# Keys of the last context made between the first scores of an attention, its values four units earlier, and one set of value copies moved to ScalarE

## The chip, the cores and the metric

The kernel runs on one core of a Trainium2 chip. The metric is device time in microseconds; before the change it is 987.43 us, the median of 3 runs (987.35 to 987.92). Engines are named as in the profile: PE (TensorE, matmul), PEld (its weight loads), DVE (VectorE), ACT (ScalarE), POOL (GpSimd), SP (the queue that issues most DMAs).

## The reference

Two layers over x of 4 batches x 512 tokens x 256 features. Each layer is an attention over a context of 1024 rows per batch and then a feed-forward with experts. The change touches the attention of the second layer and the keys and values that are made for it:

```python
# layer 1, attention (x is layer-normed first, the result is added to x)
q = (x @ Wq).reshape(B, N, H, D).transpose(0, 2, 1, 3)        # 4 heads of 64
kv = (context @ Wkv).reshape(B, M, 2, H, D).transpose(2, 0, 3, 1, 4)
k, v = (kv[0], kv[1])
attn = jnp.einsum('bhnd,bhmd->bhnm', q, k) * SCALE
attn = jnp.where(mask[:, None, :, :], attn, -jnp.inf)
attn = jax.nn.softmax(attn, axis=-1)
out = jnp.einsum('bhnm,bhmd->bhnd', attn, v)
out = out.transpose(0, 2, 1, 3).reshape(B, N, C) @ Wo
```

The feed-forward of layer 0 picks the best 2 of 12 experts for each token (8 with weights, 4 that pass the token through), that of layer 1 the best 2 of 8. All is float32.

## The kernel before

The kernel is one program in five stages: the attention of layer 0 with the routing of its tokens, the experts of layer 0, the attention of layer 1 with the routing of its tokens, four expert tiles of layer 1 ahead of time, and the experts of layer 1.

**Order of the work.** PE runs in the order in which the program is written (`manual_schedule` for PE); in the expert stages SP does too. On DVE, ACT and POOL a scheduler sets the order when the program is built, and each of these engines then runs its instructions strictly in that order. Buffers come from pools that take a tile whose last reader is done: two PSUM buffers for ordinary matmul results (`mm_ps`), two for transposes (`tr_ps`), two of two banks for scores (`score_ps`), and six of about 8 KB a partition in SBUF (`t8`) for keys, values, mask biases, row buffers and expert weights.

**Keys and values.** `mha_kv` (lines 464 to 499) is a generator that makes one batch's keys in four pieces and its values in four more. A key piece is two matmuls of 128x128 by 128x512 (L475), each in two passes, into one `mm_ps` buffer; it is copied to SBUF by ACT (L480) for the first half of the context and by DVE (L482) for the second. A value piece is four matmuls of 128x128 by 128x256 (L489); its copy goes to DVE (L495) for even pieces and to ACT (L497) for odd ones, except for batch 2, where ACT does all. `mha_kvs` chains batches. Batches 0 and 1 are made in `layer0_experts`, between the last routing steps and the first expert tile, batch 2 after the experts. Batch 3 is made inside the second attention.

**The experts of layer 0.** `moe` runs over tiles of 128 rows. For a tile `i`, `turn` forms the rows' destinations `to` on DVE (L1051, needs the rows' DMA) and transposes the rows on PE (`ht`, L1060); `up` is the first matrix (`hp`, L1085), `down` the second (`y`, L1110). Three ring slots hold expert weights; SP reloads a slot when PE has left it.

**The second attention.** `layer1_attention` (L653) goes over 32 units of (batch, 128 tokens, pair of heads), eight to a batch. Unit `i` issues: its scores (`s`, L587), whose softmax is one reduction on DVE and one exponential on ACT for each of the two heads (L596, L600); the transposes of the first head of unit `i - 2` (`a2t`, L610, copied out by DVE L613 and ACT L615); for units 11 to 18 a piece of batch 3's keys or values; the output projection (`wo`, L650) of unit `i - 4`, when it is the second pair; the values product (`o`, L635) of unit `i - 3`; a step of routing and a piece of the next batch's queries, where one is due; and last the transposes of the second head of unit `i - 2`. The scores of a unit need the score buffers of the unit before, which DVE's reduction frees. Batch 3's keys are first read in unit 24. The routing of a finished batch starts at units 11, 19 and 27 and after the last, the next batch's queries at units 0, 8 and 16, so that units eight apart lie at the same place in both.

Of the kernel before, what the change touches and what calls it, by code (L numbers as in the profile page):

```python
# [60 lines left out]
def two_layers(ctx: ExitStack, tc: tile.TileContext, io, out):  # L61
# [14 lines left out]
    def t8(shape, name, dt=F32):  # L76
        return k8.tile(shape, dt, tag="k8", name=name)
# [16 lines left out]
    def mm_ps(name):  # L94
        return ps_m.tile([P, 512], F32, tag="m", name=name)
# [41 lines left out]
    def after(a, b, why):  # L137
        info = mybir.DependencyInfo(mybir.DependencyClass.Sync, mybir.DependencyReason.DATA)
        tc.add_manual_dep(a.ins, b.ins.name, info, reason=why)
# [53 lines left out]
    for e in range(EX):  # L193
        i = nc.gpsimd.dma_start(
            out=rows[e * REGION : (e + 1) * REGION, :].rearrange("(p k) r -> p k r", p=P),
            in_=zeros.unsqueeze(1).to_broadcast([P, REGION // P, ROW]),
        )
# [264 lines left out]
    def ctx_room(k, shape, name):  # L462
        return res.tile(shape, F32, tag=f"ctxT{k}", name=name)

    def mha_kv(b, st):


        kT = ctx_room(0, [P, NC, M], "kT_2") if b == 2 else t8([P, NC, M], f"kT_{b}")
        for n in range(NC):
            for h in range(2):  # L470
                if n + h > 0:
                    yield
                op = mm_ps(f"k_{b}_{n}_{h}")
                for c in range(NC):
                    nc.tensor.matmul(  # L475
                        op, wkv[:, c, bass.ts(n, P)], ctxT[b][:, c, bass.ts(h, 512)],
                        start=(c == 0), stop=(c == NC - 1),
                    )
                if h == 0:
                    nc.scalar.copy(kT[:, n, bass.ts(h, 512)], op)  # L480
                else:
                    copied = nc.vector.tensor_copy(kT[:, n, bass.ts(h, 512)], op)  # L482
        v = ctx_room(1, [P, NJ, D], "v_2") if b == 2 else t8([P, NJ, D], f"v_{b}")
        for g in range(NJ // 2):
            yield
            op = mm_ps(f"v_{b}_{g}")
            for k in range(2):
                for c in range(NC):
                    nc.tensor.matmul(  # L489
                        op[:, bass.ts(k, D)], ctxT[b][:, c, bass.ts(2 * g + k, P)], wkv[:, c, D : 2 * D],  # L490
                        start=(c == 0), stop=(c == NC - 1),
                    )
            d = v[:, 2 * g : 2 * g + 2, :].rearrange("p j n -> p (j n)")
            if g % 2 == 0 and b != 2:
                nc.vector.tensor_copy(d, op)  # L495
            else:
                nc.scalar.copy(d, op)  # L497
        st.update(b=b, kT=kT, v=v, copied=copied)
        yield

    def mha_kvs(sts, bs):
        for b in bs:
            sts[b] = {}
            yield from mha_kv(b, sts[b])
# [6 lines left out]
    def mha_bias(st, t):  # L511

        if t == 0:
            st["mbias"] = t8([P, NT, M], f"mbias_{st['b']}", BF16)
        return nc.vector.tensor_scalar(
            st["mbias"][:, t, :], st["mask"][:, t, :], 1.0, MASKED, ALU.subtract, ALU.mult
        )
# [62 lines left out]
    def mha_scores(st, n, t):  # L580

        b = st["b"]
        sps = [score_ps(f"s2_{b}_{n}_{t}_{r}") for r in range(2)]
        for k in range(2):
            for r in range(2):
                at = slice(r * HD, r * HD + HD)
                nc.tensor.matmul(  # L587
                    sps[r][:, k, :], st["qT"][at, n, bass.ts(t, P)], st["kT"][at, n, bass.ts(k, 512)],
                    start=True, stop=True,
                )  # L590
        ps = []
        tot = sm.tile([P, 2], F32, tag="s2_tot", name=f"s2_tot_{b}_{n}_{t}", bufs=6)
        for r in range(2):
            p = t4([P, M], f"p2_{b}_{n}_{t}_{r}")
            nm = tsmall([P, 1], "s2_nm")
            nc.vector.tensor_tensor_reduce(  # L596
                p, sps[r].rearrange("p h n -> p (h n)"), st["mbias"][:, t, :],
                -ATT_SCALE, -ATT_SCALE * LEAST, ALU.add, ALU.min, nm,
            )
            nc.scalar.activation(p, p, AF.Exp, bias=nm, scale=-1.0, accum_out=tot[:, r : r + 1])  # L600
            ps.append(p)
        st["unit"] = nc.vector.reciprocal(tot, tot)
        return ps, tot
# [13 lines left out]
    def mha_turns(st, n, t, ps):  # L617
        b = st["b"]
        aT = tbig(f"a2T_{b}_{n}_{t}").rearrange("p (r k) s -> p r (k s)", r=2)
        for r, p in enumerate(ps):  # L620
            yield aT
            mha_turn(aT[:, r, :], p, f"a2t_{b}_{n}_{t}_{r}", r)
        yield
# [22 lines left out]
    def mha_out(st, t):  # L646
        b = st["b"]
        op = mm_ps(f"wo_{b}_{t}")[:, 0:D]
        for c in range(NC):
            nc.tensor.matmul(op, st["oT"][:, c, :], wo[:, c, :], start=(c == 0), stop=(c == NC - 1))  # L650
        nc.vector.tensor_tensor(x[b][:, t, :], op, x[b][:, t, :], ALU.add)

    def layer1_attention(sts):  # L653

        units = []
        for b in range(NB):
            units += [(b, t, n) for t in range(NT) for n in range(NC)]
        ps, aTs = {}, {}  # L660
        route, queries = None, None
        kvs = mha_kvs(sts, (NB - 1,))
        done = None
        for i in range(len(units) + 4):
            if i < len(units):
                b, t, n = units[i]
                ps[i] = mha_scores(sts[b], n, t)
                unit = sts[b]
                if i + 1 < len(units) and units[i + 1][0] > 0 and units[i + 1][2] == 0:
                    bias = mha_bias(sts[units[i + 1][0]], units[i + 1][1])  # L670
                    after(bias, done, "a piece to a unit")
                done = sts[b]["unit"]
            if 0 <= i - 2 < len(units):
                b, t, n = units[i - 2]
                turns = mha_turns(sts[b], n, t, ps[i - 2][0])
                aTs[i - 2] = next(turns)
                next(turns)
            if 11 <= i < 19:
                next(kvs)
            if 0 <= i - 4 < len(units):  # L680
                b, t, n = units[i - 4]
                if n == NC - 1:
                    mha_out(sts[b], t)
            if 0 <= i - 3 < len(units):
                b, t, n = units[i - 3]
                mha_values(sts[b], n, t, aTs.pop(i - 3), ps.pop(i - 3)[1])
            if route:
                next(route, None)
            if pending:
                scatter_pending(2, unit["unit"] if i < len(units) else None)  # L690
            if queries:
                next(queries, None)
            if 0 <= i - 2 < len(units):
                next(turns)
            b = i // (2 * NT) + 1
            if b < NB and i % (2 * NT) == QUERIES:
                queries = mha_q_pieces(b, sts)
            if i == len(units) - 5:
                slots = slots_ahead()
            if i == len(units) - 3:  # L700
                tiles = tiles_ahead(slots, *load_ahead(), sts[NB - 1]["unit"])
            if i == len(units) + 2:
                next(tiles)
            b, k = divmod(i - 11, 2 * NT)
            if k == 0 and 0 <= b < NB:
                route = route_steps(L1, b)
                next(route)
        for n in PIECES:
            for _ in range(n):
                next(tiles, None)  # L710
            next(route, None)
            if len(L1.run) == NB and L1.table is None:
                L1.table = tile_table(L1)
        for _ in tiles:
            pass
        return slots
# [55 lines left out]
    def scatter_pending(n, behind=None):  # L772
        for f, k, t in pending[:n]:
            i = f(k, t)
            if behind is not None:
                after(i, behind, "a few scatters with each unit")
        del pending[:n]
# [439 lines left out]
    def slots_ahead():  # L1217
        slots = {}
        for s in (0, 2):
            slots[s] = slot1(s)  # L1220
            for part in range(2):
                ring_load(L1, slots[s], part, slice(L1.first[s], L1.first[s] + 1))
        return slots
# [177 lines left out]
```

## Time and profile before

| What | Value |
|---|---|
| Median of 3 runs | 987.43 us |
| Profiled execution, its own time | 984.93 us |
| Its span, first to last instruction | 982.9 us |
| Mean granted PE clock | 0.971 |
| Batch 1's values to the first expert tile | 273.9 to 284.6 us |
| Second attention, units 0 to 31 | 416.46 us to about 694 us |

The columns of the windows that are shown later: the stretch in us, its length, busy time of the engine with the number of its instructions in brackets, granted PE clock as a share of full speed, busy share of the 16 DMA engines, GB/s.

| us from the start of the span | PE busy | DVE | ACT | PE clock |
|---|---|---|---|---|
| 250 to 275 | 23.88 | 17.98 | 3.73 | 1.00 |
| 275 to 300 | 21.87 | 5.39 | 4.84 | 0.93 |
| 400 to 425 | 21.65 | 18.82 | 11.86 | 1.00 |
| 425 to 450 | 21.18 | 14.70 | 15.78 | 0.93 |
| 450 to 475 | 24.59 | 13.48 | 13.11 | 1.00 |
| 525 to 550 | 24.67 | 15.31 | 11.30 | 1.00 |
| 550 to 575 | 23.39 | 15.56 | 13.83 | 1.00 |

A passing note for reading: a PE that waits inside a group of matmuls is shown as one longer group, so durations such as 3.03 us for scores that take 1.99 us elsewhere hold a wait.

### The profile page before, as it was taken

The page shows a single profiled execution, that of the slowest core. Times are in us where ns is not written, and L with a number is a line of the kernel's source. Part 1 is how long each engine was busy: PE and PEld are TensorE (multiplying, and loading weights), DVE is VectorE, ACT ScalarE, POOL GpSimd, SP SyncE. Part 2 cuts the span into 40 slices and gives each one's busy share as a digit, 9 for nine tenths or more (in the row PEclk, how much of TensorE's full clock was granted, in tenths as well). Part 3 has the DMA queues.
Part 4 walks back from the last instruction along what each step waited for, and adds up shares of the span by engine and source line. Part 5 has one row for each costly group of instructions (what it writes and reads, how often), then busy time and mean ns, then how long its engine had stood idle before and what let it go on. Part 6 is the DMA issues. An engine that isn't in the chain of part 4 may idle for free.

```text
span 982.9 us, 15181 instructions
## 1 busy us (share of the span) xinstructions
PE 902.5 (92%) x5506; PEld 672.3 (68%) x5506; DVE 439.6 (45%) x1262; ACT 328.7 (33%) x727; POOL 227.1 (23%) x275
## 2 busy tenths in 40 slices
PE   5888999988989999989989989989899999999995
PEld 2445464645569899546656655656778999999995
DVE  6455474544732322665664765756461211112110
ACT  2222221221111111365673464555332322323321
POOL 3310103040512222000130141133642112221121
PEclk9898999989999999999999999999989999999998
DMA  9999901211139797600000111220325868578971
GB/s 317 288 259 236 284 2 34 84 51 43 46 93 303 227 298 272 222 22 2 23 1 1 29 49 62 90 98 23 108 81 150 277 198 270 175 238 269 292 243 19
DMA packets 54907, 142.05 MB, mean 145 GB/s; under 512 B 6775, under 2 KB 32814, under 8 KB 48681
## 3 DMA queue, kind: packets, MB, share of 16 engines
q1 hardware_dynamic: 39144, 102.89, 31.4%
q0 software_dynamic: 15392, 38.10, 15.2%
q8 instruction: 47, 0.77, 0.3%
q14 instruction: 36, 0.29, 0.1%
q10 hardware_dynamic: 288, 0.00, 0.0%
HBM read 131.51 MB, written 39.91 MB: 174 GB/s over the span
## 4 chain that ended last, share of the span: by engine, by line
PE 46%; DVE 4%; ACT 4%; issue 4%; DMA 1%; another core or an unknown queue 0%; POOL 0%; POOLq 0%; ACTq 0%; DVEq 0%
PE hp L1085 11%; PE y L1110 10%; PE s L587 6%; PE a2t L610 5%; PE o L635 4%; DVE p L596 2%; ACT p L600 2%; PE y_ahead L1110 2%; PE hp_ahead L1085 1%; DMA out<-yw,to 1%; PE q L571 1%; PE v L489 1%; PE k L475 1%; PE b L934 1%; PE lgT L834 1%
## 5 line engine op out<-in xcount | busy, mean ns | idle before, releaser
L1094 ACT ACTIVATE aT<-hp,w1s 128x128 f32<-128x128 f32 x248 | 67.6, 383 | 159.2 <-issue 159.2
L1085 PEld LDWEIGHTS hp<-hT,w1s 128*128 128x128 f32 x992 | 115.6, 192 | 3.5 <-DVE hT L1066 1.9
L1085 PE MATMUL hp<-hT,w1s 128*128 128x128 f32 x992 | 116.2, 275 | 1.4 <-DVE hT L1066 1.4
L1110 PE MATMUL y<-w2s,aT 128*128 128x256 f32 x496 | 112.0, 379 | 0.0
L596 DVE CUSTOM_DVE_ANT_0 p<-s,mbias 128x1024 f32<-128x1024 f32 x64 | 75.8, 1221 | 54.0 <-PE s L587 53.9
L1110 PEld LDWEIGHTS y<-w2s,aT 128*128 128x128 f32 x496 | 91.9, 190 | 11.2
L600 ACT ACTIVATE p<-p,s_nm 128x1024 f32<-128x1024 f32 x64 | 73.5, 1148 | 66.1 <-DVE s_nm L596 66.1
L1127 POOL DMA_INDIRECT out<-yw,to x31 | 47.8, 1542 | 178.2 <-DVE to L1051 90.6
L610 PEld LDWEIGHTS a2t<-ident,p 128*128 128x128 f32 x512 | 56.9, 143 | 44.9 <-issue 22.1
L1114 DVE TENSOR_SCALAR yw<-y,row 128x256 f32<-128x256 f32 x59 | 28.6, 484 | 125.4 <-PE y L1110 125.4
L610 PE MATMUL a2t<-ident,p 128*128 128x128 f32 x512 | 72.8, 283 | 12.2 <-ACT a2T L615 5.8
L894 POOL DMA_INDIRECT rows<-rowbuf,rt_posi x64 | 65.2, 1019 | 77.5 <-DVE rt_posi L874 19.7
L587 PE MATMUL s<-kT,q2T 64*128 64x512 f32 x256 | 68.9, 642 | 2.1 <-DVE s_nm L596 2.1
L635 PE MATMUL o<-a2T,v 128*64 128x128 f32 x1024 | 63.3, 276 | 1.7 <-ACT kT L480 1.1
L331 PE MATMUL hq<-a0T,ctxn 128*128 128x512 f32 x128 | 63.0, 649 | 0.5 <-DVE a0T L265 0.5
L635 PEld LDWEIGHTS o<-a2T,v 128*64 128x64 f32 x1024 | 55.4, 137 | 11.5 <-issue 7.5
L615 ACT COPY a2T<-a2t 128x512 f32<-128x512 f32 x96 | 53.7, 581 | 23.0 <-PE a2t L610 22.7
L301 PE MATMUL s<-ctxT,q0T 128*128 128x512 f32 x128 | 59.8, 613 | 0.5 <-DVE q0T L279 0.5
L1066 DVE TENSOR_SCALAR hT<-ht,w1s 128x128 f32<-128x128 f32 x62 | 22.6, 406 | 81.7 <-PE ht L1060 76.0
L1085 PEld LDWEIGHTS hp<-hT,w0s 128*128 128x128 f32 x448 | 54.2, 192 | 3.3 <-DVE hT L1062 2.0
L1085 PE MATMUL hp<-hT,w0s 128*128 128x128 f32 x448 | 54.8, 276 | 1.1 <-DVE hT L1062 1.0
L1110 PE MATMUL y<-w0s,aT 128*128 128x256 f32 x224 | 52.8, 379 | 0.0
(259 smaller groups left out, 1245.7 us busy)
## 6 DMA issues: line engine op xcount, KB each, us to landing
w1s<-in_w1p SPq DMA_DIRECT2D x34, 1030.0 KB
w2s<-in_w2p SPq DMA_DIRECT2D x34, 1024.0 KB
rows<-zeros POOLq DMA_DIRECT2D x8, 2064.0 KB
w0s<-in_w1p SPq DMA_DIRECT2D x31, 512.0 KB
w0s<-in_w2p SPq DMA_DIRECT2D x31, 512.0 KB
row<-rows SPq DMA_DIRECT2D x59, 129.0 KB
ctxT<-in_ctxT SPq DMA_DIRECT2D x4, 1024.0 KB
ctxn<-in_ctx SPq DMA_DIRECT2D x4, 1024.0 KB
```

The source lines that it names most:

```text
L301: nc.tensor.matmul(sp[:, h, :], st["qT"][:, c, bass.ts(t, P)], ctxT[b][:, c, bass.ts(h, 512)], start=(c == 0), stop=(c == NC - 1),)
L331: nc.tensor.matmul(op, ctxn[b][:, j, bass.ts(c, P)], aT[:, j, :], start=(j == 0), stop=(j == NJ - 1))
L587: nc.tensor.matmul(sps[r][:, k, :], st["qT"][at, n, bass.ts(t, P)], st["kT"][at, n, bass.ts(k, 512)], start=True, stop=True,)
L596: nc.vector.tensor_tensor_reduce(p, sps[r].rearrange("p h n -> p (h n)"), st["mbias"][:, t, :], -ATT_SCALE, -ATT_SCALE * LEAST, ALU.add, A ...
L600: nc.scalar.activation(p, p, AF.Exp, bias=nm, scale=-1.0, accum_out=tot[:, r : r + 1])
L610: nc.tensor.transpose(pt[:, bass.ts(j, P)], p[:, bass.ts(4 * g + j, P)], ident)
L615: nc.scalar.copy(d, pt)
L635: nc.tensor.matmul(op[r * HD : r * HD + HD, :], st["v"][:, j, bass.ts(2 * n + r, HD)], aT[:, r, bass.ts(j, P)], start=(j == 0), stop=(j == ...
L894: i = nc.gpsimd.indirect_dma_start(out=rows[:, :], out_offset=bass.IndirectOffsetOnAxis(ap=pos_i[:, k, t : t + 1], axis=0), in_=buf[:, k, ...
L1085: nc.tensor.matmul(o, w1[:, c * ff + f * P : c * ff + f * P + P], hT[:, c, :], start=(c == 0), stop=(c == NC - 1),)
L1094: nc.scalar.activation(aT[:, f, :], hp[:, f // 4, bass.ts(f % 4, P)], AF.Gelu_apprx_tanh, bias=w1[:, at : at + 1])
L1110: nc.tensor.matmul(op, aT[:, f, :], w2[:, f * D : f * D + D], start=(f == 0), stop=(f == nf - 1))
```

## The change

1. In `mha_kv` batch 1's value copies all go to ACT, as those of batch 2 do.
2. In `layer1_attention` three key pieces of batch 3 are issued directly after the scores of units 0, 1 and 2, and the fourth in unit 2, ahead of the second head's transposes.
3. The pieces that units 11 to 14 issue are now the four value pieces; units 15 to 18 issue none.

```diff
@@ mha_kv
             d = v[:, 2 * g : 2 * g + 2, :].rearrange("p j n -> p (j n)")
-            if g % 2 == 0 and b != 2:
+            if g % 2 == 0 and b not in (1, 2):
                 nc.vector.tensor_copy(d, op)
             else:
                 nc.scalar.copy(d, op)
@@ layer1_attention
                 done = sts[b]["unit"]
+            if i < 3:
+                next(kvs)
             if 0 <= i - 2 < len(units):
                 b, t, n = units[i - 2]
                 turns = mha_turns(sts[b], n, t, ps[i - 2][0])
                 aTs[i - 2] = next(turns)
                 next(turns)
-            if 11 <= i < 19:
+            if 11 <= i < 15:
                 next(kvs)
...
             if pending:
                 scatter_pending(2, unit["unit"] if i < len(units) else None)
+            if i == 2:
+                next(kvs)
             if queries:
                 next(queries, None)
             if 0 <= i - 2 < len(units):
                 next(turns)
```

The scheduler sets ACT's and DVE's order anew around the moved pieces. In the changed program: ACT runs both exponentials of unit 2, then the copy of the third key piece, then the second half of the first transposes' copies, then the square-root table and its use, then the copies of the second head's transposes. The first mask bias of batches 1 and 2 (DVE) moves from before the reductions of units 7 and 15 to behind them. In unit 18 ACT's copy of `combT` stands ahead of the square-root table instead of behind it. The order on POOL and SP is as before.

## The prediction

> **What bounds the kernel now.** I read the page's busy shares first, then busy time and granted clock in 25 us stretches, then the timeline of the three places that the diff touches, TensorE (PE) first.
>
> ```profile
> PE 902.5 (92%) x5506; PEld 672.3 (68%) x5506; DVE 439.6 (45%) x1262; ACT 328.7 (33%) x727; POOL 227.1 (23%) x275
> ```
>
> PE is busy for 92% of the span; VectorE (DVE) and ScalarE (ACT) have more than half of theirs free. So time falls where PE loses a wait, half-clock time, or work that has a gap to lie in elsewhere. Timeline rows are: start, duration, engine, line, operation, count, and in brackets the idle time before and what ended it. The values of batch 1, ahead of the first experts:
>
> ```profile
> 277.51 0.59 ACT L497 COPY v<-v 128x512 f32<-128x512 f32 x1 [4.58 <-PE v L489]
> 278.70 0.22 DVE L1051 SCALAR_TENSOR_TENSOR to<-row,tt_valid,tt_aside 128x1 int32<-128x1 f32 x1 [3.94 <-DMA row<-rows]
> 278.83 0.68 DVE L495 COPY v<-v 128x512 f32<-128x512 f32 x1
> 279.57 5.01 PEld L489 LDWEIGHTS v<-wkv,ctxT 128*128 128x128 f32 x16 [2.50 <-DVE v L495]
> 279.57 5.41 PE L489 MATMUL v<-wkv,ctxT 128*128 128x256 f32 x16 [2.09 <-DVE v L495]
> 284.82 0.38 PE L1060 MATMUL ht<-ident,row 128*128 128x128 f32 x2
> ```
>
> The copy of the first values stands on DVE behind a `to` that waits for the first rows (until 278.70). PE's third value piece needs the PSUM buffer of the first and so loses 2.09 us. The 16 passes after it then take 5.4 us, the 16 before 3.6. The clock column (fourth figure) of the 1 us windows says why:
>
> ```profile
> 278.00:279.00 1.00, 0.00 (x0) 1.00 0.49 131
> 281.00:282.00 1.00, 1.00 (x4) 0.50 0.00 0
> 282.00:283.00 1.00, 1.00 (x4) 0.50 0.00 0
> 284.00:285.00 1.00, 1.00 (x7) 1.00 0.12 36
> ```
>
> The start of the second attention, PE alone:
>
> ```profile
> 416.46 1.99 PE L587 MATMUL s<-kT,q2T 64*128 64x512 f32 x8
> 419.86 3.03 PE L587 MATMUL s<-kT,q2T 64*128 64x512 f32 x8 [1.41 <-DVE s_nm L596]
> 423.55 3.12 PE L587 MATMUL s<-kT,q2T 64*128 64x512 f32 x8 [0.66 <-DVE s_nm L596]
> 426.61 1.09 PE L610 MATMUL a2t<-ident,p 128*128 128x128 f32 x8
> 429.90 1.30 PE L610 MATMUL a2t<-ident,p 128*128 128x128 f32 x8 [2.20 <-ACT a2T L615]
> 431.14 3.42 PE L587 MATMUL s<-kT,q2T 64*128 64x512 f32 x8
> ```
>
> Units 0 to 2 bring PE 1.99 us of scores each and start 3.4 to 3.7 us apart: the score buffers wait for DVE's reduction. A 2.20 us gap follows, and the scores of unit 3 take 3.42 us for 1.99, with the clock at 0.50 again from 431 to 434. Later units are different. Unit 15 (with a value piece) and unit 23, eight later at the same place in the routing (without):
>
> ```profile
> 533.12 1.99 PE L587 MATMUL s<-kT,q2T 64*128 64x512 f32 x8
> 535.03 1.09 PE L610 MATMUL a2t<-ident,p 128*128 128x128 f32 x8
> 535.96 1.89 PE L489 MATMUL v<-wkv,ctxT 128*128 128x256 f32 x8
> 537.69 1.03 PE L650 MATMUL wo<-wo,oT 128*128 128x256 f32 x4
> ...
> 610.17 1.99 PE L587 MATMUL s<-kT,q2T 64*128 64x512 f32 x8
> 612.08 1.09 PE L610 MATMUL a2t<-ident,p 128*128 128x128 f32 x8
> 613.01 1.03 PE L650 MATMUL wo<-wo,oT 128*128 128x256 f32 x4
> ```
>
> PE goes from piece to piece without a wait there: a piece removed is time removed.
>
> **Part A, the copies of batch 1's values.** DVE loses two copies of 0.69, ACT gains two of 0.59. ACT idles 4.58 us before its copy at 277.51 and 6.92 us before its next, so nothing on ACT is late. The first piece ends near 275.7, ACT has copied it near 276.5, and PE wants the buffer at 277.5. So the 2.09 us wait goes. Without the gap I also expect no half clock: from 279.57 to the next stage's weight load at 284.60 are 5.03 us, two pieces at full speed are 3.46 (16 passes of 0.216, from the row before). That is 1.57 more: **-3.7**. Next late would be the first tile's `ht`, which wants the rows landed by 278.70; PE comes at about 281, so that wait does not take its place. Tile weights are requested when PE frees a ring slot and follow it.
>
> [...] The rows show half clock beginning within 1 us after gaps of 2.09 and 2.20 us; I go by the rows.
>
> **Part B, four key pieces into units 0 to 2.** Each is two matmuls in four passes, 1.72 to 1.88 us of PE. The first two go behind the scores of units 0 and 1. PE is free from about 418.4 and 422.5, and the second of the next four score matmuls has to wait for DVE until 420.91 and 424.69 anyway; the piece ends at about 420.1 and 424.2. Cost about 0. Their copies (0.59 on ACT, 0.69 on DVE) fall in idle time of 1.36 and 1.31 us ahead of the next exponential and reciprocal. The third runs to about 428.2, and the transposes of unit 0 move behind it. Then comes the fourth. On ACT the changed order has both exponentials of unit 2, the key copy, and only then the second half of the transposes' copies, which before came between the exponentials. From 428.2: two exponentials to 430.85, key copy to 431.45, transposes' copy to 432.0. The last four transposes wait for that and end at 432.8; unit 3's scores start there instead of at 431.14, at full clock, and end at about 434.7 instead of 434.5. The square-root and exponential tables (1.28 each) now have two copies between them, so that ACT is free at 436.0; its exponential began at 435.86 before. I carry **+0.3**. Cover gone (half clock stays): +1.5 more. Lower end -0.5, if the waits are shorter than I make them.
>
> **Part C, units 11 to 14** have value pieces instead of key pieces: the same PE time. The copy changes engine each time (ACT, DVE, ACT, DVE becomes DVE, ACT, DVE, ACT). In unit 13 PE waited 1.13 us for ACT's key copy at 516.17; on DVE the copy follows the transposes' and should end about 0.75 earlier. In unit 12 ACT gets 0.59 more in a stretch where it sets the pace with its table loads. I take **-0.5**, ends -1.3 and +0.7.
>
> **Part D, units 15 to 18** lose a value piece each. Start-to-start of the scores against the twins 23 to 26: 11.28 - 9.44, 7.71 - 6.08, 9.08 - 7.24, 9.91 - 7.46, that is 1.84 + 1.63 + 1.84 + 2.45 = **-7.8**. The last is more than a piece because PE stood 1.56 us for `combT` behind ACT's square-root table; the changed order on ACT has `combT` first. The lower end is four pieces of 1.75 = 7.0 less 1 for a pace set by others.
>
> **What moves beside it.** Batch 3's keys and values take their SBUF buffers earlier, so the first mask bias of batches 1 and 2 (DVE, 0.68) moves behind the reduction of units 7 and 15, into the buffer of the finished batch's keys. Behind it stands the transposes' copy (467.18); its buffer is wanted at 470.46, so over 2 us cover it: 0. Without the cover it is 0.7 twice. No DMA is added, removed or moved on SP or POOL; the early weight load on SP gets one more wait, for PE work that is long done.
>
> **Sum.** -3.7 + 0.3 - 0.5 - 7.8 = -11.7. The profiled execution took 984.93 us (span 982.9): 973.2. The timed runs have a median 2.5 above it, so the same difference from 987.43 gives **975.7**.
>
> **The rivals.**
> 1. *Another engine paces units 15 to 18.* A unit without extras cannot be shorter than its chain: scores 2.0, two reductions 2.4, DVE copy 0.7, transposes 1.0 = 6.1, which is what unit 24 takes. Against it: units 15 and 17 have more PE work than that. If half of D is lost: 979.6.
> 2. *The half clock stays*[...]: A is worth 2.1 and B costs 1.8, so 987.43 - 2.1 + 1.8 - 8.3 = 978.8.
> 3. *Slower: the clock.* PE with less to do from unit 15 on has more short gaps; before, 578 to 580 and 647 to 649 each lost some 1.1 us and were followed by half clock. A stretch costs about 1.7 us (3.4 at half speed). Seven more in the 17 units 15 to 31 eat the whole gain; with nine it is 987.43 - 11.7 + 15.3 = 991. Against it: units 24 to 26, built as 16 to 18 will be, show none.
> 4. *Nothing is moved that counts*, since the softmax paces all of the attention: only A remains, 983.7. The unbroken PE rows of unit 15 speak against it.
>
> **How the numbers follow.** Mine 0.68 (own range 973 to 978.5: A ±0.5, B -0.5 to +1.8, C ±1, D ±1, half-clock stretches elsewhere ±1.7). Rival 1 0.12, rival 2 0.12, rival 4 0.04, rival 3 0.04, of which 0.01 stops within 0.2% (2 us, about what a measurement here can tell from no change). The range 971.5 to 980.5 takes in the first two rivals. Faster 0.96, same 0.01, slower 0.03.
>
> **What would show it.** A: no wait before the third value piece, clock 1.0 there, first `ht` near 281. B: key pieces between the scores, the clock full around 431, unit 3's scores beginning near 432.8 less A's gain. C: the 1.13 us wait gone. D: units 15 to 18 starting about 9.4, 6.1, 7.2 and 7.5 us apart. I am wrong if half-clock stretches come up in the units between, or if the first four units take over 1 us longer.

## The result and the profile after

The changed kernel takes 975.77 us (median of 4 runs, 974.84 to 976.8), the kernel before 987.67 beside it (4 runs, 987.35 to 989.21). The ratio is 0.9877, with a 95% interval of 0.9854 to 0.9900: 12.1 us less, between 9.9 and 14.4. The forecast was 975.7.

The profiled execution took 975.56 us (span 973.6), only 9.4 less than the profiled one before (984.93). PE's share, in the page's busy times:

```profile
PE 902.0 (93%) x5506; PEld 674.4 (69%) x5506; DVE 440.0 (45%) x1260; ACT 329.5 (34%) x729; POOL 227.0 (23%) x275
```

PE's work is the same 5506 matmuls; the span around them is shorter. Part A in the timeline of PE (start, duration, engine, line, operation, count):

```profile
274.72 7.07 PE L489 MATMUL v<-wkv,ctxT 128*128 128x256 f32 x32
281.63 0.38 PE L1064 MATMUL ht<-ident,row 128*128 128x128 f32 x2
```

The same stretch in the timeline of ACT (behind the count: idle before, and what ended it):

```profile
277.12 0.59 ACT L497 COPY v<-v 128x512 f32<-128x512 f32 x1 [3.33 <-PE v L489]
278.38 0.59 ACT L497 COPY v<-v 128x512 f32<-128x512 f32 x1 [0.67 <-PE v L489]
```

All four value pieces are one unbroken group of 7.07 us. From its start to the first `ht` are 6.91 us, where 273.86 to 284.82 were 10.96. The clock over it (fourth figure) stays full:

```profile
278.00:279.00 1.00, 1.00 (x6) 1.00 0.45 132
281.00:282.00 1.00, 1.00 (x6) 1.00 0.00 0
```

Part B, the start of the second attention in the timeline of PE:

```profile
412.33 1.99 PE L587 MATMUL s<-kT,q2T 64*128 64x512 f32 x8
414.24 1.98 PE L475 MATMUL k<-ctxT,wkv 128*128 128x512 f32 x4
416.16 2.60 PE L587 MATMUL s<-kT,q2T 64*128 64x512 f32 x8
418.69 1.98 PE L475 MATMUL k<-ctxT,wkv 128*128 128x512 f32 x4
420.60 1.99 PE L587 MATMUL s<-kT,q2T 64*128 64x512 f32 x8
422.52 1.98 PE L475 MATMUL k<-ctxT,wkv 128*128 128x512 f32 x4
424.34 1.04 PE L610 MATMUL a2t<-ident,p 128*128 128x128 f32 x8
425.21 1.88 PE L475 MATMUL k<-ctxT,wkv 128*128 128x512 f32 x4
426.93 1.35 PE L610 MATMUL a2t<-ident,p 128*128 128x128 f32 x8
428.22 1.99 PE L587 MATMUL s<-kT,q2T 64*128 64x512 f32 x8
```

The clock at the former half-clock place:

```profile
428.00:430.00 2.00, 2.00 (x11) 1.00 0.00 0
```

The key pieces fill what were waits, but for a short wait inside unit 1's scores (2.60 us for 1.99). Unit 3's scores begin 15.89 us after unit 0's (14.68 before) but run at full clock, and unit 4's begin 22.67 us after unit 0's (22.89 before). Part D, unit 15:

```profile
527.18 1.99 PE L587 MATMUL s<-kT,q2T 64*128 64x512 f32 x8
529.10 1.09 PE L610 MATMUL a2t<-ident,p 128*128 128x128 f32 x8
530.03 1.03 PE L650 MATMUL wo<-wo,oT 128*128 128x256 f32 x4
530.99 1.97 PE L635 MATMUL o<-a2T,v 128*64 128x128 f32 x32
```

The piece is gone and nothing waits in its place.

This table of stages serves all that follows. It gives, for the profiled execution of each kernel, the time from the first value piece of batch 1 to the first `ht`, then from the scores of one unit to those of another (us).

| Kernel | values to `ht` | units 0-4 | 4-11 | 11-15 | 15-19 | 19-21 | 21-27 | 27-31 |
|---|---|---|---|---|---|---|---|---|
| before | 10.96 | 22.89 | 51.24 | 42.53 | 37.98 | 20.01 | 49.28 | 35.93 |
| changed | 6.91 | 22.67 | 51.39 | 40.79 | 30.55 | 20.00 | 49.27 | 39.18 |
| changed, second | 6.90 | 22.68 | 51.39 | 40.79 | 30.55 | 20.01 | 49.27 | 37.54 |
| changed, third | 6.90 | 22.67 | 51.40 | 40.79 | 30.54 | 21.64 | 49.28 | 37.62 |
| A alone | 6.91 | 22.88 | 51.18 | 42.53 | 37.99 | 20.00 | 49.27 | 37.26 |
| gap filled | 9.20 | 23.97 | 51.22 | 42.54 | 37.98 | 18.37 | 49.27 | 39.24 |
| all but A | 10.97 | 22.68 | 51.40 | 40.78 | 30.55 | 18.36 | 49.26 | 39.24 |
| keys alone | 10.85 | 22.67 | 51.38 | 34.76 | 37.99 | 21.24 | 49.28 | 37.63 |
| keys twice | 11.05 | 22.68 | 51.38 | 42.53 | 37.98 | 20.01 | 49.27 | 37.58 |
| copies exchanged | 6.91 | 22.68 | 51.38 | 42.54 | 30.54 | 19.69 | 49.28 | 37.65 |
| transposes first | 6.91 | 22.68 | 51.39 | 40.79 | 30.54 | 18.32 | 49.28 | 33.78 |
| the same, second | 6.90 | 22.68 | 51.39 | 40.79 | 30.54 | 18.32 | 49.27 | 37.09 |
| late values | 6.91 | 22.67 | 51.38 | 37.42 | 30.54 | 19.91 | 49.28 | 35.88 |

Most columns repeat to a few hundredths for the same order of work, so a profile tells much smaller differences here than whole times do. Executions differ by some us between `ht` and unit 0 (130.5 to 135.8 us), in units 19 to 21 (18.36 to 21.64 for one order of work), in units 27 to 31 and in what comes before the values. Units 0 to 4 in the order of before took 22.88 and 22.89 us, and once 23.97 (gap filled).

The changed parts sum to -4.05 - 0.22 + 0.15 - 1.74 - 7.43 = **-13.3 us**, the same in all three profiles of the changed kernel. In the first one, units 27 to 31 took 39.18 us for 35.93, which hides 3.25 of it.

### The profile page after: what moved, and what is told of

Its sections match the earlier page's. It is cut to its first block, busy times and chain, and to the rows that moved or that the text cites. A ratio compares the mean times of both kernels' runs of the same rounds, so it can differ in the third digit from the quotient of the medians.

```text
span 973.6 us, 15188 instructions
## 1 busy us (share of the span) xinstructions
PE 902.0 (93%) x5506; PEld 674.4 (69%) x5506; DVE 440.0 (45%) x1260; ACT 329.5 (34%) x729; POOL 227.0 (23%) x275
## 4 chain that ended last, share of the span: by engine, by line
PE 45%; DVE 5%; issue 4%; ACT 4%; DMA 1%; another core or an unknown queue 1%; POOL 0%; POOLq 0%; ACTq 0%; DVEq 0%
PE hp L1089 11%; PE y L1114 10%; PE s L587 6%; PE a2t L610 5%; PE o L635 4%; ACT p L600 2%; PE y_ahead L1114 2%; DVE p L596 1%; PE q L571 1%; DMA out<-yw,to 1%; PE hp_ahead L1089 1%; PE wo L650 1%; PE v L489 1%; PE lgT L838 1%; PE k L475 1%
## 5 line engine op out<-in xcount | busy, mean ns | idle before, releaser
L331 PE MATMUL hq<-a0T,ctxn 128*128 128x512 f32 x128 | 60.5, 627 | 0.0
```

The source lines that it names most:

```text
L331: nc.tensor.matmul(op, ctxn[b][:, j, bass.ts(c, P)], aT[:, j, :], start=(j == 0), stop=(j == NJ - 1))
```

## The experiments

The later runs lay on other chips, on which the kernel before takes 980 to 983 us; the part behind unit 31 takes 302 to 303 us in their profiles, and 306.6 and 307.5 in the first two. So absolute expectations are read as differences, and whole times only as ratios to the kernel before on the same chip.

### A alone

```diff
@@ kernel before
-            if g % 2 == 0 and b != 2:
+            if g % 2 == 0 and b not in (1, 2):
```

> The kernel before with batch 1's value copies on ScalarE, nothing else. My theory (a wait of 2.09 us and the half clock after it both go): 3.7 to 3.8 us less than before, about 983.9. Rival (only the wait goes, the slow clock has another cause and comes back elsewhere in the stage): about 2.1 less, 985.6. Rival (the first tile waits for something else anyway): no change.

Measured: ratio 0.9968 (0.9951 to 0.9985), 3.2 us less, between 1.5 and 4.8. The stage itself lost 4.05 us, and up to unit 27 no later stage gave it back (units 27 to 31, which differ between executions, took 37.26 us for 35.93). The interval alone would not exclude 2.1; the stage does.

### The gap filled with spare work

Two matmuls that nobody reads, where PE waits; the wait on DVE's copy stays.

```diff
@@ kernel before, mha_kv
         for g in range(NJ // 2):
             yield
+            if b == 1 and g == 2:
+                fill = score_ps("fill")
+                for k in range(2):
+                    nc.tensor.matmul(fill[:, k % 2, :], wkv[:, 0, 0:P], ctxT[b][:, 0, 0:512], start=True, stop=True)
             op = mm_ps(f"v_{b}_{g}")
```

> The kernel before with two spare matmuls of 128x512 on TensorE (1.7 us, their result is read by nobody) between batch 1's second and third value piece, where TensorE waits 2.09 us; the copies stay where they were, so the wait itself stays. Theory (the short gap brings the half clock): the clock stays full there and about 1.6 us go, 986.0. Rival (a gap of 2 us is too short to matter for the clock): no change, 987.6, and half clock from 281 to 284 as before.

Measured: ratio 0.9984 (0.9972 to 0.9997), 1.6 us less. PE's timeline of this kernel:

```profile
272.41 3.62 PE L493 MATMUL v<-wkv,ctxT 128*128 128x256 f32 x16
275.86 1.88 PE L489 MATMUL fill<-ctxT,wkv 128*128 128x512 f32 x4
278.05 3.72 PE L493 MATMUL v<-wkv,ctxT 128*128 128x256 f32 x16 [0.31 <-DVE v L499]
281.61 0.38 PE L1064 MATMUL ht<-ident,row 128*128 128x128 f32 x2
```

Windows of 1 us of the same kernel, the clock as fourth figure:

```profile
278.00:279.00 1.00, 0.95 (x4) 1.00 0.00 0
279.00:280.00 1.00, 1.00 (x6) 1.00 0.06 16
280.00:281.00 1.00, 1.00 (x7) 1.00 0.00 0
```

The third piece still waits for DVE, as late as before. With the gap filled, the 16 passes behind it take 3.72 us instead of 5.41, and the stage 9.20 instead of 10.96. The half clock came from the 2 us gap here: in all four profiles in which that gap stands (before 2.09 us, all but A 2.12, keys alone 1.99, keys twice 2.19) the 16 passes behind it take 5.41 us. It made 1.8 of A's 4.05 us.

### All but A

```diff
@@ changed kernel
-            if g % 2 == 0 and b not in (1, 2):
+            if g % 2 == 0 and b != 2:
```

> The changed kernel with batch 1's value copies as before (even ones on VectorE). Theory (the parts add up): 3.7 to 3.8 us more than the changed kernel, about 979.5. Rival (the attention hides part of it): under 2.5 us more.

Measured: ratio 0.9926 (0.9901 to 0.9951), against 0.9865 (0.9837 to 0.9893) for the changed kernel on the same chip: 6 us apart, with about 4 of uncertainty. Whole times can't say more than that A is not lost. By stages it is 4.07 us, and the attention is as in the changed kernel until unit 19, so the parts add.

### The changed kernel again

> The changed kernel once more, for its spread and a second profile. Median 975.8. Theory: units 0 to 26 take the same time to 0.5 us as in the first profile of it; units 27 to 31 differ[...]. Rival (the 3.2 us that units 19 to 31 lost in the first profile belong to the change): the same loss, s of unit 19 to s of unit 31 again about 108.4 us against 105.2 before.

Measured: ratio 0.9865 (0.9837 to 0.9893). Units 0 to 27 take the same to 0.02 us, units 27 to 31 37.54 us instead of 39.18. Unit 19 to unit 31 took 106.8 us, between the rival's 108.4 and the 105.2 of before, so the loss did not repeat as it was. Nor is it tied to the change: in units 27 to 31 kernels whose order there is that of before took 35.93, 37.26, 37.58 and 39.24, and the changed kernel 39.18, 37.54 and 37.62.

### Keys at the start, values where they were

```diff
@@ kernel before, layer1_attention
                 done = sts[b]["unit"]
+            if i < 3:
+                next(kvs)
...
-            if 11 <= i < 19:
+            if 15 <= i < 19:
                 next(kvs)
...
+            if i == 2:
+                next(kvs)
             if queries:
```

> The kernel before with the keys of batch 3 in units 0 to 2 as in the change; its values stay in units 15 to 18, so that units 11 to 14 have no piece at all. Value copies of batch 1 as before. Theory (a piece removed from a full TensorE is time removed, wherever it was): 7 us less from units 11 to 14 and about 0.2 from the start, 980.4. Rival (ScalarE with its table loads and the waits for buffers pace units 11 to 13, so only part comes out): 3.5 us less, 984.

Measured: ratio 0.9944 (0.9923 to 0.9965), 5.5 us less, between 3.4 and 7.6, which does not exclude the rival's 3.5. Units 11 to 15 lost 7.77 us, so by stages the theory stands and "half of it" does not. But the four units differ: 1.03, 2.12, 2.89 and 1.73 us for a piece of 1.72 to 1.82. In unit 11 a new wait appears:

```profile
498.65 0.60 PE L610 MATMUL a2t<-ident,p 128*128 128x128 f32 x4
500.30 0.66 PE L610 MATMUL a2t<-ident,p 128*128 128x128 f32 x4 [1.05 <-ACT a2T L615]
```

The transposes of the second head come earlier and meet ACT, which loads two tables (1.28 us each, at 493.99 and 496.11) ahead of the exponentials and the copy: the rival's mechanism, in one unit of four. In units 12 and 13 more than the piece goes: in unit 13 the wait of 1.13 us behind it goes too, and in unit 12 two waits of 0.48 and 0.66 become one of 0.80.

### Keys made twice

```diff
@@ the same, but the pieces of units 11 to 18 stay, and the keys of batch 3 are made two times
-        for n in range(NC):
+        for n in list(range(NC)) * (2 if b == 3 else 1):
...
             if 11 <= i < 19:
                 next(kvs)
```

> The kernel before with batch 3's keys made twice: in units 0 to 2 as in the change, and again in units 11 to 14 as before (the second writes the same numbers over the first). It measures what the four pieces cost at the start. Theory (they lie in waits, and the full clock pays for the rest): 987.4, within 0.5 us of before. Rival (they take their TensorE time): 7 us more, 994.6.

Measured: ratio 1.0009 (0.9979 to 1.0039), and from unit 4 to unit 27 every stage is as before to 0.14 us; units 0 to 4 take 22.68 us. Four pieces, 7 us of PE work, cost -0.2 us there. The rival's +7 us would be 1.007.

### Value copies on the other engines

```diff
@@ changed kernel
-            if g % 2 == 0 and b not in (1, 2):
+            if g % 2 == (1 if b == 3 else 0) and b not in (1, 2):
```

> The changed kernel with the engines of batch 3's value copies exchanged, so that units 11 to 14 copy on ScalarE, VectorE, ScalarE, VectorE as the key pieces did before. Theory (the gain in units 11 to 14 is the copy's engine): units 11 to 14 take 1.7 us more than in the changed kernel, 977.5. Rival (the gain there comes from the changed order of other work): no change, 975.8.

Measured: ratio 0.9889 (0.9842 to 0.9935), too wide for this. Units 11 to 15 take 42.54 us, to 0.01 what the key pieces took. PE in unit 13, first here, then of the changed kernel:

```profile
510.74 1.03 PE L650 MATMUL wo<-wo,oT 128*128 128x256 f32 x4
512.88 1.97 PE L635 MATMUL o<-a2T,v 128*64 128x128 f32 x32 [1.12 <-ACT v L497]
```

```profile
509.15 1.03 PE L650 MATMUL wo<-wo,oT 128*128 128x256 f32 x4
510.22 1.97 PE L635 MATMUL o<-a2T,v 128*64 128x128 f32 x32
```

The values product needs the PSUM buffer that the piece left, and ACT copies late (at 512.26) because its two exponentials stand before the copy. In the changed kernel DVE copies at 509.49, and the wait is gone wholly. All of part C is this choice of engine: 0.47 us in unit 11, 0.21 in unit 12, 1.07 in unit 13.

### The second head's transposes ahead of the bias step

In units 19 and 27 `next(turns)` moves ahead of the step of routing that adds fc2_b.

```diff
@@ changed kernel, layer1_attention
+            early = i in (19, 27)
+            if early:
+                next(turns)
             if route:
                 next(route, None)
...
-            if 0 <= i - 2 < len(units):
+            if 0 <= i - 2 < len(units) and not early:
                 next(turns)
```

> The changed kernel; in units 19 and 27 the transposes of the second head are issued before the routing step with the expert bias (fc2_b) instead of behind it, so that TensorE has work where it waited 1.09 and 0.78 us and half clock followed. Theory (short gaps bring the half clock): 1.9 us of waits and 1.7 to 3.4 us of half clock each go in part, 971 to 973. Rival (the waits go, half clock stays): 974. Rival (the wait only moves behind the transposes): 975.8.

> The changed kernel with the second head's transposes ahead of the bias step in units 19 and 27, timed beside the changed kernel. Theory (two waits and three to four half-clock stretches gone): s of unit 19 to s of unit 31 again about 101.4 us, 5 us less than the changed kernel; in time about 0.5% less than it. Rival (the first profile was a lucky one): 105 or more, no difference.

Measured: ratios 0.9864 (0.9817 to 0.9910) and 0.9866 (0.9832 to 0.9901); the changed kernel beside the second, run once more for this:

> The changed kernel, to be timed on one chip beside the next two, with a third profile. Theory from the stage times of the profiles so far (4.05 us from the value copies, 0.2 from the start, 1.7 from units 11 to 14, 7.4 from units 15 to 18): 13.4 us or 1.36% less than before. Rival (part of it is lost again to half clock in units 27 to 31, as in the first profile): 10 us, 1.0%.

It had 0.9895 (0.9866 to 0.9923). The intervals overlap, so in whole times the gain is not shown. In stages, units 19 to 21 take 18.32 us both times against 20.0 to 21.6 of the changed kernel. But two kernels with the old order there, gap filled and all but A, took 18.37 and 18.36, with unit 20's scores at 2.0 us, while these took 2.79, 3.26 and 3.55 us in the changed kernel's three profiles. The wait of 1.09 us only moved: it stands inside the transposes now, as 1.05 us, much as the last rival had it. In unit 27 the new order is worth 0.55 us (9.40 for 9.95 without half clock, in copies exchanged); the rest of the difference is half clock that did not come in the first profile, where the scores of units 27 to 31 all took 1.99 us. Unit 19 to unit 31 was expected at 101.4 again and took 101.4 and then 104.7, against 106.8 to 108.5 of the changed kernel. So the second expectation failed by 3.3 us, which lie in units 28 and 29 (scores of 3.66 and 3.38 us for 1.99). The same transposes there in PE's timeline of the first profile, and the window behind them, the clock as fourth figure:

```profile
643.14 0.66 PE L610 MATMUL a2t<-ident,p 128*128 128x128 f32 x4 [1.81 <-ACT a2T L615]
```

```profile
645.00:646.00 1.00, 1.00 (x7) 1.00 0.37 132
```

The same two views of the second profile:

```profile
648.92 0.66 PE L610 MATMUL a2t<-ident,p 128*128 128x128 f32 x4 [1.81 <-ACT a2T L615]
```

```profile
651.00:652.00 1.00, 1.00 (x6) 0.50 0.19 66
```

The same wait of 1.81 us in the same kernel is followed by full clock once and by half clock once.

As for the changed kernel's third run: 1.05% less, between 0.77 and 1.34. The 1.36% of its theory lies just outside, its rival's 1.0% inside. In its profile units 19 to 21 lost 1.6 us more to half clock than in the two before it (`b`, transposes and scores took 1.96, 1.97 and 3.55 us, in the first profile 1.13, 1.92 and 2.79), so of the gain before unit 19 part can be lost again in an execution, as its rival has it, though at another place.

### Values in the waits

As the last kernel, and the value pieces of units 12, 13 and 14 go to units 12, 13 and 20, behind the query piece.

```diff
@@ transposes first
-            if 11 <= i < 15:
+            if i == 11:
                 next(kvs)
...
+            if i in (12, 13, 20):
+                next(kvs)
             if 0 <= i - 2 < len(units) and not early:
                 next(turns)
```

> As the run before it, and the last three value pieces of batch 3 stand in units 12, 13 and 20 behind the query piece, where TensorE waits for a copy, instead of in units 12, 13 and 14 ahead of the values product. Theory (a piece in a wait costs its time less the wait: 0.7, 0.4 and 0.8 us): 1.5 to 2 us less than the run before in units 11 to 20. Rival (the piece delays the copies that the transposes wait for, so that the wait comes back behind it): no gain.

Measured: ratio 0.9838 (0.9800 to 0.9876); 963.48 us beside 967.69 for the kernel it builds on and 970.66 for the changed kernel, all on one chip. It is the shortest of the three; its interval still touches both others'. Units 11 to 21 take 1.79 us less than in the kernel it builds on (87.87 against 89.66), the expected number, but by luck: half clock (0.50 from 566 to 569) fell on unit 20, whose scores took 3.62 us for 1.99. Without it the three moved pieces would have saved about 3.4 us, an estimate from the 1.79 and the 1.63 that these scores lost. Unit 12:

```profile
502.05 0.66 PE L235 MATMUL xn2Tp<-ident,xn 128*128 128x128 f32 x4
502.54 1.89 PE L489 MATMUL v<-wkv,ctxT 128*128 128x256 f32 x8
504.27 1.04 PE L610 MATMUL a2t<-ident,p 128*128 128x128 f32 x8
```

The transposes used to wait here, 0.45 us for ACT's copy of the transposes before and 0.47 us for the query's (`xn2T`, on DVE) in the changed kernel, and now follow the piece without a wait.

## Why the prediction was right

The total was right, and for the most part by its own steps; that it was met to 0.1 us was luck.

**Part A**, forecast -3.7, was -4.05. Wait and half clock both went, as two separate runs show: A alone took the stage from 10.96 to 6.91 us, and with the gap filled the clock stayed at 1.00 and the 16 passes took 3.72 us for 5.41. In the profile before, PE's clock stood at 0.50 from about 280.46 to 283.87 and from 430.65 to 434.06, 3.4 us each, beginning 0.89 us after the end of the gap of 2.09 us and 0.75 us after that of 2.20. That the first tile waits for nothing new was right.

**Part B**, forecast +0.3, was -0.22. The first two pieces cost about nothing, as forecast: unit 2's scores began 1.18 us later than before, counted from unit 0's (8.27 for 7.09), but no longer waited inside, and PE was through with them at 10.19 us instead of 10.15. Unit 3's scores began 0.45 us earlier than worked out (15.89 us after unit 0's, not 16.34): unit 2's two exponentials on ACT, without a copy between them, took 2.29 us and not the 2.65 reckoned. The full clock paid for the rest: without it the pieces would have cost over a microsecond, by an estimate from the 1.43 us that unit 3's scores and the 0.21 us that the transposes ahead of them took longer at half clock before. Its worth is not fixed, though. In the gap-filled kernel, which starts the attention in the order of before, half clock came a little earlier in the work and lasted longer (the transposes, scores and transposes from 426.76 on took 1.97, 3.79 and 1.44 us, before 1.30, 3.42 and 1.10), and units 0 to 4 took 23.97 us; against that the pieces save 1.3.

Later +0.15 us appears between units 4 and 11. Unit 7 takes 8.78 us for 8.56, where the mask bias was moved behind the reduction and carried at 0, and unit 10 gives 0.05 back. The prediction looked only at the buffer of the transposes' copy. Behind that copy stands DVE's add of the output projection (L651), which now ends at 464.44, and the query's matmuls begin at 464.50. That they wait for this add fits the times but was not tested.

**Part C**, forecast -0.5, was -1.74: the mis-sized term. The wait of 1.13 us in unit 13 was taken to shrink by 0.75 and went; a loss on ACT was feared in unit 12 and did not come; unit 11's 0.46 was not looked for.

**Part D**, forecast -7.8, was -7.43. The twins gave units 15 to 17 as 9.44, 6.08 and 7.24; they are 9.47, 6.08 and 7.23. Unit 18 came to 7.77 for 7.46. ACT has `combT` first as foreseen, and PE waits for it as long as in the twin; unit 18 of the changed kernel, then unit 26 of the kernel before:

```profile
557.15 0.66 PE L610 MATMUL a2t<-ident,p 128*128 128x128 f32 x4 [0.72 <-ACT combT L933]
```

```profile
639.80 0.66 PE L610 MATMUL a2t<-ident,p 128*128 128x128 f32 x4 [0.73 <-ACT combT L929]
```

The 0.31 us lie on DVE. Its timeline in unit 18, then in unit 26 before:

```profile
549.10 0.75 DVE L549 BATCH_NORM_STATS2 ln_st<-x 128x6 f32<-128x256 f32 x2
552.30 1.22 DVE L596 CUSTOM_DVE_ANT_0 p<-s,mbias 128x1024 f32<-128x1024 f32 x1
```

```profile
634.95 1.23 DVE L596 CUSTOM_DVE_ANT_0 p<-s,mbias 128x1024 f32<-128x1024 f32 x1 [1.01 <-PE s L587]
```

In unit 18 DVE works without a break from 549.10 to the first reduction, which begins 2.34 us after the scores (549.96). In unit 26 it has time to wait for the scores, and begins 2.02 us after them (632.93). Among the work in unit 18 is the layer norm of the next batch's queries (L549); unit 26 has none, since no batch follows. So the twin lacked more than the piece, and rival 1, another engine's pace, was right for 0.3 us.

Together -13.3 instead of -11.7, so the changed parts gave 1.6 us more than forecast, and the measured 12.1 was met because something else took about as much back. **The luck**: taking the profiled execution's distance from the median as the same before and after failed. Before it was 2.5 us; after, the profiled run is within 0.3 of the median. The profile before was a favourable one: its units 27 to 31 took the least of the four in that order (35.93, the others 37.26 to 39.24). Three comparisons of whole times gave ratios of 0.9877, 0.9865 and 0.9895, 10 to 13 us; the stages' 13.3 is 1.35%. What takes some of it back varies between executions. Units 27 to 31 are one such place (35.9 to 39.2 us, in either order), as the term for "half-clock stretches elsewhere" allowed, and units 19 to 21 another. Units 19 to 31 average 106.4 us in the four profiles with the order of before and 107.5 in five with the changed order (all but A and copies exchanged among them). That would fit, but the ranges overlap (105.2 to 106.9, 106.6 to 108.5), so whether these units account for the whole difference is open.

Of the rivals, another engine's pace shows in units 15 to 18 only in the 0.31 us of unit 18, the half clock did not stay at either place, and the softmax does not pace the middle of the attention. More half-clock stretches (the slower rival) did come in the first profile, 3.25 us of them net, but not from a PE with less to do: units 21 to 27 never lose a microsecond (49.26 to 49.28 us in all 13 profiles), and kernels with the order of before lose as much (39.24 us in the gap-filled one).

## What to carry to other kernels

Work that fills a short wait on the bound engine can gain twice: its own time where it was, and the clock that the wait may have cost. Here four key pieces, 7 us of PE work, made units 0 to 4 0.2 us shorter. A copy belongs on the engine whose queue reaches it first: of two copies with nearly the same duration (0.59 and 0.69 us) the slower engine was better in one place (unit 13, where 1.12 us of wait went) and the faster one in the other (batch 1's values, where 2.09 us went), because of what stood ahead. For units that repeat, take the twin without the piece as the forecast; it was right to 0.03 us in three of four. Then list what else the unit has and the twin has not, on every engine: in the fourth that was 0.31 us.

## What was not expected of the hardware

The half clock does not follow the length of a wait alone. After the same 1.81 us in unit 28 it came once and not once in one kernel, as shown above. This wait stands in 11 of the 13 profiles: in two (before, and transposes first) the scores behind it took 1.99 us, in the other nine 3.1 to 3.5 us. In the kernel before, a wait of 1.56 us (unit 18) was followed by full clock (1.00 from 571 to 574), and one of 0.78 us (unit 27) by half clock (0.50 from 650 to 652). In the second profile of the transposes-first kernel it set in near 640 us (0.86 from 639 to 640, 0.50 from 640 to 643), where the only wait in the 3 us before was 0.38 us, between two groups of `b` (L941).

What else decides is not shown: no run varied the instant of a wait.
